# The last steps of a graph layer on one core: stores of the output without an order, and the work behind the last gather in another order

## The chip, the cores and the metric

The kernel runs on one core of a Trainium2 chip. The core has a matrix engine (TensorE, in the profile PE, with PEld for the loads of its stationary operand), a vector engine (VectorE, DVE), a scalar engine (ScalarE, ACT), GpSimd (POOL) and a sync engine (SyncE, SP), each with an instruction stream of its own; 16 DMA engines move data between the chip's DRAM and its SBUF. PE writes into PSUM, eight banks of 2 KB per partition, from which DVE and ACT read. The metric is the device time of one execution in microseconds (us); less is better. The time before the change is the median of three runs.

## What is computed

A graph attention layer over N = 12500 nodes of 256 features (HID) in 8 heads of D = 32, and E = 200000 edges sorted by their target `dst`. `src` gives the edge's other end.

```python
h = relu(layernorm(x))                                  # over the 256 features
q, k, v = h @ Wq + bq, h @ Wk + bk, h @ Wv + bv         # per node, 8 heads of 32
logits = einsum('ehd,ehd->eh', q[dst], k[src]) / sqrt(32)
expv = exp(logits - segment_max(logits, dst)[dst])
attn = expv / segment_sum(expv, dst)[dst]
agg = segment_sum(attn[:, :, None] * v[src], dst)
y = h + gelu(agg.reshape(N, 256) + h @ Wskip + bskip)
out = x + layernorm(y) * gamma + beta
```

## The kernel before

**Stages.** `project` computes h, k and v for all nodes and writes them to tables in DRAM (`h_tab`, `kv_tab`); beside it `make_plan` prepares the edges. Then `walk_streams` walks the edges, and this is nearly all of the time. The list of edges is cut into S = 8 streams of 25000, and 66 steps (NST) each take 383 edges of every stream, in K = 3 tiles of 128 edges. The last step, 65, has two tiles. An edge's row of `kv_tab` is gathered by an indirect DMA on POOL (`gather_row`, L1041), 128 rows at a time, eight for a tile; the tile lies in a buffer named `kv`, of which there are six.

**A step** c, for its tiles j:

- `spread` (L1092, PE) spreads the queries of the step's window of nodes over the edges; `times` (L1102, DVE) multiplies by k, in two halves; `total` (L1109, DVE) sums to logits.
- `turn` (L1125, PE) turns the logits of tile j into the bank `ps_x`, the one bank for the logits and the weights of all steps; `maxima` (L1137 to L1140 on DVE, then the exponential, L1141, on ACT) finds the maximum of each node and takes the exponential; `turn_back` (L1147, PE) turns the weights back into the same bank.
- `weights` (L1155, L1157, ACT) copies weights into the buffers `vw`, of which there are three; `weigh` (L1164, DVE) multiplies v by the weights into `vw`; for tile 0 there is L1169 besides.
- `hot_n` (L1082, ACT, behind a product on PE) makes `to_n`, which says which edge belongs to which node. There is one buffer for it.
- `add_up(c, i)` (L1183, PE) sums the weighted rows by node, in three groups i of streams: group 0 has the four streams with a narrow window (32 nodes), groups 1 and 2 two wide ones (64) each. ACT copies the sums to SBUF (L1193, one copy for a group) and hands each stream's open node on to the next step, one copy for a stream (L1199: four, two and two). SP stores the sums to `table` (L1203): four, two and two stores.

The stages of two steps are interleaved by hand: while step c is weighed and added up, the logits of step c + 1 are made.

**Finished nodes** are taken in pairs of blocks of 128 nodes (`Pair`), a pair in about four of five steps from step 10 on; pair 45 is the one that is started in step 64. A pair goes through `fetch` (SP: sums from `table`, x, and h), `turn` (h transposed on PE, L825, and copied by ACT to `hT`, L828), `skip` (h @ Wskip, on PE: bias L838 and eight products L842), `divisors` and `divide` (DVE, L817 to L831), `add` (PE adds the quotient to the skip product, L847), `gelu` (ACT, L851), `stats` (DVE, L854 to L860), `root` (ACT, L864), `factors` (DVE), `normal` (ACT, L874), `shifted` (PE, x + beta, L881 and L884), `scale` (DVE, L888 and L890: the result) and two `store` (SP, L895). ACT needs the table of Gelu, of Sqrt or of Exp for three of these functions; `table_of` (L963) calls for one ahead of its use with a one-element dummy.

**The last four pairs**, 46 to 49, can only be summed when the last step is done. They are of the class `Last`: x and h are fetched early (`fetch_rows`, L918 and L919), into two `kv` buffers that no gather needs any more, two pairs in each; the sums come behind the last store to `table` (`find_sums` reads the places, `fetch_sums`, L926, loads). Their skip products lie in the four banks `ps_qe`, which are those of `spread`. Two further pairs are behind a branch that isn't taken with these inputs.

**What sets the order.** Buffers, semaphores and waits are placed by a framework, from the tiles that each instruction reads and writes. It serializes writes into one DRAM tensor whose place is known only at run time, as the stores to `out` are; `table` has a place per stream. The order of the instructions on PE, DVE, ACT and SP is that of the program's text: `keep` ties each instruction to the one before it on its engine.

Behind the loop, in step 65, the text before does in this order: `hot_n`, `maxima`, pair 45's quotient, `turn_back`, `weights`, `weigh` of tile 0, pair 45 up to gelu, the first last pair's `turn`, `add_up` of tile 0, `weigh` of tile 1, `add_up` of tile 1, `skip` of the first last pair, the fetch of the sums, the rest of pair 45, `turn` and `skip` of the other three, the stores of the two pairs in flight, then the last four pairs from `divisors` on, stage by stage.

## Time and profile before

| what | value |
|---|---|
| time, median of 3 runs | 2327.23 us (2321.52 to 2327.32) |
| the profiled execution's own time | 2328.28 us |
| its span, first to last instruction | 2326.5 us |
| DVE busy | 1922.8 us, 83% |
| PE busy | 1816.3 us, 78% |
| POOL busy | 1561.7 us, 67% |
| ACT busy | 1066.4 us, 46% |
| DMA engines, mean rate over the span | 257 GB/s |
| mean granted clock of PE | 0.889 |
| last gather issued (POOL) | at 2241.76 us |

The span is cut by the loop: up to about 2242 us the gathers run, and from there to the end, 84 us, is the stage that the change is about. Rows of the instructions in order of time begin with the start in us from the span's start and the duration in us; then engine, line, operation, what is written and read, shape and count. In brackets stands how long the engine was idle before it and what ended that. A row with a count covers several instructions in a row, from the first's start. Rows by source line give minimum, median and maximum duration in ns, and the first and last start.

### The profile page before, as it was taken

To read this page: it belongs to the slowest core of one execution; us is meant where nothing else is said; L and a number is where in the kernel's file an instruction comes from. 1 tells how busy PE (TensorE), PEld (TensorE's weight loads), DVE (VectorE), ACT (ScalarE), POOL (GpSimd) and SP (SyncE) were. 2 spreads that over 40 slices of the span, in tenths; PEclk is the share of its full clock that TensorE was granted. 3 is DMA by queue.
4 is the path that set the end of the run, shared out by engine and by line. 5 is a ranking of instruction groups with operands and counts; after the bars stand their busy time and mean duration, and the time that the engine had idled before them with its cause. 6 is when DMAs were issued, how large, how long until landed. Compare 5 with 4: busy or idle time off the path is not lost.

```text
span 2326.5 us, 36089 instructions
## 1 busy us (share of the span) xinstructions
PE 1816.3 (78%) x10196; PEld 1070.9 (46%) x10196; DVE 1922.8 (83%) x2205; ACT 1066.4 (46%) x2517; POOL 1561.7 (67%) x1648
## 2 busy tenths in 40 slices
PE   7899666677788788788788788788787888788775
PEld 3444334444445454445454444455454545445443
DVE  8889477777888888888899888888898888799874
ACT  3432223333355455455455455455454555455453
POOL 2220677777777777777777777777777777777740
PEclk9999778888798899898899899898899899899887
DMA  7866788888889899898988888998998898898871
GB/s 285 290 243 222 238 235 244 243 244 243 260 267 277 258 275 276 263 274 266 274 272 271 264 267 264 270 274 261 275 277 265 266 274 264 263 276 267 265 214 54
DMA packets 275990, 597.92 MB, mean 257 GB/s; under 512 B 52295, under 2 KB 166164, under 8 KB 273600
## 3 DMA queue, kind: packets, MB, share of 16 engines
q0 software_dynamic: 128768, 423.23, 60.7%
q1 hardware_dynamic: 146482, 171.81, 22.7%
q8 instruction: 84, 1.38, 0.2%
q14 instruction: 126, 1.03, 0.1%
q10 hardware_dynamic: 530, 0.47, 0.1%
HBM read 512.83 MB, written 82.47 MB: 256 GB/s over the span
## 4 chain that ended last, share of the span: by engine, by line
PE 35%; DMA 23%; DVE 17%; ACT 12%; issue 7%; POOL 5%; SPq 1%; DVEq 0%; ACTq 0%; POOLq 0%
DMA kv<-kv_tab,idx 21%; DVE vw L1164 7%; PE ps_qe L1092 6%; PE ps_kv L250 5%; PE ps_a L1183 5%; PE ps_hot L1183 4%; PE ps_hot L1021 4%; DVE L L1109 4%; PE ps_a L842 4%; DVE kv L1102 4%; POOL kv L1041 3%; ACT kv L1199 3%; ACT to_n L1082 3%; PE ps_a L847 1%; ACT sums_w L1193 1%
## 5 line engine op out<-in xcount | busy, mean ns | idle before, releaser
L1041 POOL DMA_INDIRECT kv<-kv_tab,idx x1528 | 1471.5, 963 | 465.5 <-issue 220.3
L1102 DVE TENSOR_TENSOR kv<-ps_qe,kv 128x1024 f32<-128x1024 f32 x394 | 471.5, 1220 | 270.4 <-DMA kv<-kv_tab,idx 167.4
L1092 PE MATMUL ps_qe<-qw,to_e 64*128 64x256 f32 x3152 | 454.1, 420 | 108.3 <-DVE kv L1102 78.9
L1164 DVE TENSOR_TENSOR vw<-ps_x,kv 128x2048 f32<-128x2048 f32 x197 | 449.5, 2282 | 28.8 <-ACT vw L1157 28.1
L1109 DVE TENSOR_REDUCE L<-kv 128x64 f32<-128x2048 f32 x197 | 450.0, 2284 | 5.2
L1092 PEld LDWEIGHTS ps_qe<-qw,to_e 64*128 64x128 f32 x3152 | 328.6, 203 | 246.8 <-issue 150.1
L1024 ACT COPY qw<-ps_hot 128x256 f32<-128x256 f32 (+1 forms) x132 | 63.3, 479 | 429.7 <-PE ps_hot L1021 429.7
L1183 PE MATMUL ps_a<-vw,to_n 128*32 128x264 f32 (+1 forms) x2344 | 245.4, 441 | 11.2 <-ACT kv L1199 10.8
L1007 ACT COPY hwT<-ps_hot 128x256 f32<-128x256 f32 (+1 forms) x132 | 63.5, 481 | 343.9 <-PE ps_hot L1003 343.7
L1021 PE MATMUL ps_hot<-w_q,hwT 128*128 128x256 f32 x792 | 212.1, 405 | 1.0 <-ACT hwT L1007 0.8
L250 PE MATMUL ps_kv<-w_kv,hT 128*128 128x512 f32 x392 | 185.1, 615 | 22.9 <-ACT hT L143 22.0
L1021 PEld LDWEIGHTS ps_hot<-w_q,hwT 128*128 128x128 f32 x792 | 143.3, 194 | 82.2 <-issue 57.2
L1125 PE MATMUL ps_x<-ident,L 128*64 128x128 f32 x197 | 60.5, 307 | 151.4 <-DVE vw L1164 135.7
L963 ACT ACT_TABLE_LOAD x138 | 177.1, 1283 | 2.5
L1183 PE MATMUL ps_hot<-vw,to_n 128*64 128x264 f32 x808 | 155.2, 540 | 1.8 <-DVE o L890 1.8
L1183 PEld LDWEIGHTS ps_a<-vw,to_n 128*32 128x32 f32 (+1 forms) x2344 | 101.9, 130 | 98.1 <-issue 28.7
L1199 ACT COPY kv<-ps_a 1x264 f32<-1x264 f32 x388 | 143.2, 369 | 6.4
L1070 ACT ACTIVATE to_e<-ps_hot,ones 128x384 f32<-128x384 f32 x264 | 142.2, 582 | 6.2 <-DMA wide<-gvu_d 6.1
L1193 ACT COPY sums_w<-ps_a 128x264 f32<-128x264 f32 x130 | 49.3, 379 | 180.7 <-PE ps_a L1183 177.7
L842 PE MATMUL ps_a<-w_s,hT 128*128 128x256 f32 x368 | 120.4, 484 | 14.8 <-ACT hT L828 13.7
L250 PEld LDWEIGHTS ps_kv<-w_kv,hT 128*128 128x128 f32 x392 | 71.7, 193 | 105.5 <-issue 70.6
L1067 PE MATMUL ps_hot<-et,near 48*128 48x384 bf16 x264 | 86.5, 328 | 41.3 <-ACT qw L1024 26.6
(282 smaller groups left out, 2103.5 us busy)
## 6 DMA issues: line engine op xcount, KB each, us to landing
kv<-kv_tab,idx POOLq DMA_INDIRECT x1576
kv_tab<-kvo SPq DMA_DIRECT2D x14, 1536.0 KB
hw<-h_tab SPq DMA_DIRECT2D x264, 64.0 KB
table<-sums_w SPq DMA_DIRECT2D x264, 61.9 KB
pen<-pen_tab SPq DMA_DIRECT2D x66, 192.5 KB
sums<-table SPq DMA_DIRECT2D x92, 132.0 KB
x_f<-in_x_dram SPq DMA_DIRECT2D x92, 128.0 KB
h<-h_tab SPq DMA_DIRECT2D x92, 128.0 KB
```

The costliest lines, as they stand in the source:

```text
L250: ins = nc.tensor.matmul(ps_kv, hT[:, c, :], w_kv[:, c, :], start=c == 0, stop=c == KC - 1)
L842: self.keep(nc.tensor.matmul(self.ps[:, b, :], self.hT[:, b, c, :], w_s[:, c, :], start=False, stop=False, skip_group_check=True))
L963: keep(nc.scalar.activation(dummy[:, 1:2], dummy[:, 0:1], function))
L1021: keep(nc.tensor.matmul(ps[:, b, :], g["hwT"][:, b, k, :], w_q[:, k, :], start=False, stop=k == KC - 1, skip_group_check=True))
L1041: ins = nc.gpsimd.indirect_dma_start(out=t[:, s, :], out_offset=None, in_=kv_tab[:, :], in_offset=bass.IndirectOffsetOnAxis(ap=idx[:, s, j ...
L1070: keep(nc.scalar.activation(step[c]["to_e"][:, i, :], ps[:, :CH], AF.Relu, scale=-1.0, bias=ones))
L1092: keep(nc.tensor.matmul(ps[:, b, a, :], g["to_e"][r, 2 * half + a, j * P:(j + 1) * P], g["qw"][r, (half + a) * half, :], start=True, stop= ...
L1102: keep(nc.vector.tensor_tensor(k, g["qe", half].rearrange("p b a d -> p a b d"), k, op=OP.mult))
L1109: keep(nc.vector.tensor_reduce(g["L"][:, j, :].rearrange("p (s h) -> p s h", s=S), g["kv"][j][:, :, :HID].rearrange("p s (h d) -> p s h d" ...
L1164: keep(nc.vector.tensor_tensor(t[:, :, HEADS:].rearrange("p s (h d) -> p s h d", h=HEADS), wj[:, :, :, None].to_broadcast([P, S, HEADS, D] ...
L1183: keep(nc.tensor.matmul(ps[at:at + w, :], g["to_n"][:, j, i * P + at:i * P + at + w], g["vw"][j][:, s, :], start=j == 0, stop=j == tiles_o ...
L1199: keep(nc.scalar.copy(step[c + 1]["kv"][0][0:1, s, HID - HEADS:], ps[at:at + 1, :]))
```

## The change

Three things are changed, all in `walk_streams`.

1. The stores to `out` are declared free of dependencies on one another (two blocks of nodes can overlap, and a node's row is the same in both). This holds for all pairs.
2. In step 64 the rows of the first two last pairs are fetched earlier in SP's order, ahead of the turn of step 64's last logits; their `turn` and `skip` stand ahead of the weighing of step 64's tile 1 and of the turn of step 65's tile 1.
3. What stands behind the loop is put into another order. Step 64 breaks off after the weighing of its last tile. Then come the Exp table, `add_up(64, 0)`, `maxima(65)`, `add_up(64, 1)`, `turn_back(65)`, `add_up(64, 2)`, `hot_n(65)`; tile 1 is weighed before `weights`, then pair 45 up to the quotient, then tile 0. Each group is added up for both tiles at once. Pair 44 (`older`) and pair 45 (`pair`) go through `stats` to `scale` together, so that one Sqrt table serves both; the third last pair's `turn` and `skip` stand between `root` and `factors`, the fourth's behind the next Gelu table. `products` allocates the `vw` buffers apart from `weights`.

No arithmetic is added or removed; behind the start of step 64 there is one load of a table less on ACT (a Sqrt).

```diff
         def store(self, b):
...
-            self.keep(nc.sync.dma_start(out[ds(self.nodes[b], P), :], self.y[:, b, :]))
+            ins = self.keep(nc.sync.dma_start(out[ds(self.nodes[b], P), :], self.y[:, b, :]))
+            tc.declare_no_dep(ins.ins, group="stores", reason="a node's row is the same in every block")
+            tc.add_to_no_dep_group("stores", ins.ins)
...
+        def products(c):
+            step[c]["vw"] = [work.tile([P, S, SUMS], F32, name="vw", bufs=K) for _ in range(K)]
...
             if c:
                 weigh(c - 1, K - 1)
                 gather_next(c - 1, K - 1)
+            if c == NST - 2:
+                for i in range(2):
+                    last(i)
             if c + 2 < NST:
                 turn_windows(c + 2, 0)
             turn(c, K - 1)
...
             if c == NST - 2:
-                for i in range(4):
+                for i in range(2, 4):
                     last(i)
...
             total(c + 1, 1)
+            if c == NST - 2:
+                for p in lasts[:2]:
+                    p.turn()
+                    p.skip()
             weigh(c, 1)
             gather_next(c, 1)
             turn(c + 1, 1)
...
             if c == NST - 2:
                 weigh(c, K - 1)
-                add_up(c, 0, range(K - 1, K))
-                add_up(c, 1)
-                if pair_next:
-                    pair_next.turn()
-                    pair_next.skip()
+                older, pair, before = pair, pair_next, None
+                break
             if pair:
                 table_of(AF.Sqrt)
                 pair.stats()
                 pair.root()
                 table_of(AF.Exp)
-            if c == NST - 2:
-                add_up(c, 2)
...
         c = NST - 1
+        n = tiles_of(c)
+        table_of(AF.Exp)
...
+        add_up(c - 1, 0, range(K - 1, K))
+        maxima(c)
+        add_up(c - 1, 1)
+        turn_back(c)
+        add_up(c - 1, 2)
+        for j in range(n):
             hot_n(c, j)
+        products(c)
+        for j in range(1, n):
+            weigh(c, j)
+        weights(c)
         if pair:
+            pair.turn()
+            pair.skip()
             pair.divisors()
             pair.divide()
         weigh(c, 0)
+        table_of(AF.Gelu)
         if pair:
             pair.add()
             pair.gelu()
+        if older:
+            older.stats()
         for p in lasts:
             p.find_sums()
         for i in range(3):
+            add_up(c, i, range(n))
         for p in lasts:
             p.fetch_sums()
         if pair:
             pair.stats()
+        table_of(AF.Sqrt)
+        for p in (older, pair):
+            if p:
+                p.root()
+        for p in lasts[2:3]:
             p.turn()
             p.skip()
+        for p in (older, pair):
+            if p:
+                p.factors()
+                p.normal()
+        for p in (older, pair):
+            if p:
+                p.shifted()
+        table_of(AF.Gelu)
+        for p in lasts[3:]:
+            p.turn()
+            p.skip()
+        for p in (older, pair):
             if p:
+                p.scale()
                 p.store(0)
                 p.store(1)
```

More of the change, by code (lines that the diff above doesn't have):

```diff
@@ L1149, in turn_back @@
             turns(latest[PE])
+        def products(c):
+            step[c]["vw"] = [work.tile([P, S, SUMS], F32, name="vw", bufs=K) for _ in range(K)]
         def weights(c):
             g = step[c]
-            g["vw"] = [work.tile([P, S, SUMS], F32, name="vw", bufs=K) for _ in range(K)]
+            if "vw" not in g:
+                products(c)
             keep(nc.scalar.copy(wden[c % 2][0:1], g["kv"][0][0:1, :, HID - HEADS:HID]))
@@ L1374, in walk_streams @@
         c = NST - 1
-        for j in range(tiles_of(c)):
-            if tiles_of(c) == K and j < 2:
-                times(c, K - 1, j)
-            hot_n(c, j)
-            if tiles_of(c) == K and j == 1:
-                total(c, K - 1)
-        if tiles_of(c) == K:
-            turn(c, K - 1)
-        maxima(c)
+        n = tiles_of(c)
+        table_of(AF.Exp)
+        if n == K:
+            for half in range(2):
+                times(c, K - 1, half)
+            total(c, K - 1)
+            turn(c, K - 1)
+        add_up(c - 1, 0, range(K - 1, K))
[4 more added lines that the diff above has]
+        for j in range(n):
+            hot_n(c, j)
+        products(c)
+        for j in range(1, n):
+            weigh(c, j)
+        weights(c)
         if pair:
-            table_of(AF.Gelu)
+            pair.turn()
+            pair.skip()
             pair.divisors()
             pair.divide()
-        if before:
-            before.factors()
-        turn_back(c)
-        weights(c)
         weigh(c, 0)
+        table_of(AF.Gelu)
         if pair:
@@ L1395, in walk_streams @@
             pair.gelu()
-        if before:
-            before.normal()
-            before.shifted()
-        for p in lasts[:1]:
-            p.turn()
-        for j in range(1, tiles_of(c) - 1):
-            weigh(c, j)
-        for i in range(3):
-            add_up(c, i, range(tiles_of(c) - 1))
-        weigh(c, tiles_of(c) - 1)
+        if older:
+            older.stats()
         for p in lasts:
@@ L1408, in walk_streams @@
         for i in range(3):
-            add_up(c, i, range(tiles_of(c) - 1, tiles_of(c)))
-        for p in lasts[:1]:
-            p.skip()
-        if before:
-            before.scale()
+            add_up(c, i, range(n))
         for p in lasts:
@@ L1417, in walk_streams @@
             pair.stats()
-            pair.root()
-            pair.factors()
-            pair.normal()
-            pair.shifted()
-            pair.scale()
-            table_of(AF.Gelu)
-        for p in lasts[1:]:
+        table_of(AF.Sqrt)
[3 more added lines that the diff above has]
+        for p in lasts[2:3]:
             p.turn()
             p.skip()
-        for p in (before, pair):
+        for p in (older, pair):
             if p:
+                p.factors()
[10 more added lines that the diff above has]
+                p.scale()
                 p.store(0)
```

## The prediction

> **What bounds the kernel now.** First the head of the page, and the busy time by stretches of the last stage.
>
> ```profile
> span 2326.5 us, 36089 instructions
> ...
> 2310.00:2327.00 17.00, 0.00 (x0) 0.00 (x0) 0.00 (x0) 0.00 (x0) 0.00 (x0) 0.50 0.14 43
> ```
>
> The profiled run took 2328.28 us: its span and 1.78 us around it, 1.05 us over the median of the runs (2327.23). In the last 17 us no engine computes. So I read there the instructions in order of time (of SP too), the rows of the output's stores by tile, SP's waits, and the rows of the program's last line.
>
> ```profile
> 2309.29 0.69 DVE L890 TENSOR_TENSOR kv<-kv,ps_hot 128x512 f32<-128x512 f32 x1 [0.41 <-PE ps_hot L884]
> ...
> 2303.40 17.13 SPq L895 DMA_DIRECT2D out_dram<-kv  x8
> ...
> L895 SPq DMA_DIRECT2D out_dram<-kv x8: 332/332/333, 2303.4 to 2320.2; - x8
> ...
> SPq L895 <- DMA out_dram<-kv: 13.1, 7, 3.0
> ...
> L1800 SPq EVENT_SEMAPHORE  x14: 17/28/28, 2324.9 to 2326.4; - x14
> ```
>
> The last result is ready at 2309.29 + 0.69 = 2309.98. The eight stores of the last four pairs run from 2303.4 to 2320.2, 2.4 us apart, and seven of them waited 13.1 us in all for the store before. From the last issue to the end are 2326.5 - 2320.2 = 6.3 us: the landing, the branch, and from 2324.9 the meeting of the engines. These 6.3 us stay.
>
> Next the instructions from the turned logits of step 65 (tile 1) to the first quotient that is added.
>
> ```profile
> 2252.89 0.42 PE L1125 MATMUL ps_x<-ident,L 128*64 128x128 f32 x1 [4.97 <-DVE vw L1164]
> ...
> 2253.35 2.29 DVE L1164 TENSOR_TENSOR vw<-ps_x,kv 128x2048 f32<-128x2048 f32 x1 [0.51 <-PE ps_x L1125]
> ...
> 2255.70 1.11 PE L1183 MATMUL ps_a<-vw,to_n 128*32 128x264 f32 x8 [0.47 <-DVE vw L1164]
> ...
> 2256.90 0.38 ACT L1193 COPY sums_w<-ps_a 128x264 f32<-128x264 f32 x1 [8.40 <-PE ps_a L1183]
> ...
> 2257.17 1.55 ACT L1199 COPY kv<-ps_a 1x264 f32<-1x264 f32 x4
> ...
> 2258.58 0.42 DVE L1140 TENSOR_TENSOR W<-ps_x,M 64x256 f32<-64x256 f32 x1
> ...
> 2262.58 1.56 PE L1183 MATMUL ps_hot<-vw,to_n 128*64 128x264 f32 x12
> ...
> 2266.19 0.41 ACT L1141 ACTIVATE W<-W 64x256 f32<-64x256 f32 x1
> ...
> 2268.38 2.29 DVE L1164 TENSOR_TENSOR vw<-ps_x,kv 128x2048 f32<-128x2048 f32 x1 [5.68 <-ACT vw L1157]
> ...
> 2276.07 2.03 PE L1183 MATMUL ps_hot<-vw,to_n 128*64 128x264 f32 x8
> ...
> 2276.26 0.38 ACT L1193 COPY sums_w<-ps_a 128x264 f32<-128x264 f32 x1 [4.40 <-PE ps_a L1183]
> ...
> 2278.18 0.38 ACT L1193 COPY sums_w<-ps_hot 128x264 f32<-128x264 f32 x1 [0.50 <-PE ps_hot L1183]
> ...
> 2282.29 5.61 SPq L926 DMA_DIRECT2D kv<-table  x8
> ...
> 2285.03 0.17 DVE L817 TENSOR_SCALAR den<-kv 128x16 f32<-128x16 f32 x1 [1.82 <-DMA kv<-table]
> ...
> 2289.64 0.18 DVE L817 TENSOR_SCALAR den<-kv 128x16 f32<-128x16 f32 x1 [0.24 <-DMA kv<-table]
> ...
> 2291.87 1.03 PE L847 MATMUL ps_qe<-kv,ident 128*128 128x256 f32 x4
> ```
>
> DVE has nothing for 5.68 us before 2268.38: step 65 is weighed late, because its exponential ran at 2266.19 although its argument was there at 2258.58 + 0.42 = 2259.00. On ACT it stood behind all copies of step 64's sums, a turned h and two table loads. Step 65's sums are complete on PE at 2278.10 and copied at 2278.56, the table is read back from 2282.29, and the first quotient is added on PE at 2291.87, though its sums were there at 2285.03: PE was still at skip products of later pairs.
>
> **The change part by part.** Prices, from the instructions in order of time:
>
> ```profile
> 2204.92 4.57 SPq L1203 DMA_DIRECT2D table<-sums_w  x8
> ...
> 2247.65 0.27 PE L1125 MATMUL ps_x<-ident,L 128*64 128x128 f32 x1
> ...
> 2248.11 0.33 SPq L812 DMA_DIRECT2D h<-h_tab  x1
> ...
> 2258.82 0.66 PE L825 MATMUL ps_hot<-ident,h 128*128 128x128 f32 x4
> ...
> 2259.57 0.69 DVE L831 TENSOR_TENSOR o<-sums,den 128x512 f32<-128x512 f32 x1 [0.21 <-DVE den L819]
> ...
> 2260.02 0.59 ACT L828 COPY hT<-ps_hot 128x512 f32<-128x512 f32 x1
> 2260.62 1.28 ACT L963 ACT_TABLE_LOAD   x1
> ...
> 2265.25 1.05 ACT L1082 ACTIVATE to_n<-ps_hot,ones 128x384 f32<-128x384 f32 x2
> ...
> 2268.25 0.58 ACT L851 ACTIVATE sums<-ps_a 128x512 f32<-128x512 f32 x1
> ...
> 2280.60 1.09 ACT L874 ACTIVATE sums<-sums,nm,rstd 128x256 f32<-128x256 f32 x2 [0.43 <-DVE nm L869]
> 2280.78 1.13 PE L884 MATMUL ps_hot<-x_f,ident 128*128 128x256 f32 x4
> ...
> 2283.72 1.99 PE L842 MATMUL ps_qe<-w_s,hT 128*128 128x256 f32 x8 [1.05 <-ACT hT L828]
> ```
>
> *Two skip products ahead of the turned logits.* PE is free from 2247.65 + 0.27 = 2247.92 to 2252.89. A pair costs there 0.66 (transposes), 0.59 (copy on ACT, which is free), 1.99 (eight products) and some 0.05 between: 3.3 us; two end at 2254.5. The turned logits end at 2254.8 instead of 2253.31, and step 64's third weighing, which waited 0.51 for them before too, runs from 2254.85 to 2257.15 instead of 2255.64: 1.5 us lost on the path. In return two skip products leave the row in front of 2291.87.
>
> Those logits lie in other columns than the weights that DVE reads, and yet PE waited 4.97 us at 2252.89 for a weighing, and DVE for PE behind it. The Trainium skill, PSUM — Partial Sum Buffer, section PSUM bank collisions raise a hardware error, says that accesses of two engines are to be kept apart by bank, not by address. By this rule, with which the trace agrees, the 1.5 us are lost; by address the weighing could start at 2252.9, and the sum would be some 1.3 us better.
>
> *Exponential ahead of copies.* Step 64's first group of sums is complete 1.11 us after 2257.15 (PE's last eight products, as at 2255.70), at 2258.3; its copies (1.9 us, 2256.90 to 2257.17 + 1.55) stay in front: 2260.2. DVE's scans are done at 2259.0 as before, so the exponential ends at 2260.6 instead of 2266.60. The Sqrt table and root no longer stand before it, and the Exp table (1.28 and the dummy) is loaded while ACT is empty, about 2253. Then on PE the turned weights (0.35) and the third group of sums, 1.56, to 2262.5. That frees the buffer into which tile 1 is weighed: 2262.5 to 2264.8. ACT meanwhile: copies of two groups to 2263.6, to_n 1.05 to 2264.65, the copy of weights behind the weighing to 2265.1. Pair 45: hT to 2265.7, skip 1.99 to 2267.75, add 1.13 (four products against ident, as the shifted x) to 2268.9, gelu 0.58 to 2269.5; its Gelu table fits beside the skip. DVE has divisors and quotient (1.3) to 2266.1 and tile 0 to 2268.6, under PE's 2269.5, which must leave the bank first.
>
> *Sums in one go.* 32 products: 16 narrow ones and 16 wide ones. Wide ones at 1.56 / 12 are 2.1 us, at the rate of 2276.07 (eight in 2.03) 4.1; the narrow ones half of that. PE has little idle time there, so I take the first, 3.1 us: 2272.6, against 2278.10; the other would be 3 us worse. Gain by here 5.5 us. Its first copy ends at 2271.0; eight table stores and the fetch start 5.65 later, as before (2276.26 + 0.38 to 2282.29): 2276.7. Sums of the first pair arrive at 2279.4, of the last at 2284.0 (2.74 and 7.35 later, as 2285.03 and 2289.64).
>
> *The rest.* ACT: last copy 2273.0, Sqrt table and dummy 1.5, two roots, hT of the third pair: 2275.6. PE: its skip to 2277.7, two shifted x (1.45 each with the bias) to 2280.6, transposes of the fourth pair, hT on ACT (four normals, twice 1.09, and the Gelu table are done at 2279.3), skip: 2283.9. DVE scales pairs 44 and 45 by 2281.3 and has the first quotient at 2282.6, under PE's 2283.9. So the first add starts at 2283.9 instead of 2291.87: 8.0 us less, 2.5 more than by the sums. What follows to the last result, 2309.98 - 2291.87 = 18.1 us, is unchanged: 2302.0.
>
> *Stores in any order.* The last two go out at 2302.0 and 2302.6 (0.6 us each, as eight table stores in 4.57), not at 2320.2: 17.6 less, of which 9.6 would come with the old order of work (2309.98 and one 0.6 for 2320.2). The end: 2302.6 + 6.3 = 2308.9. In the loop such waits are next to nothing (the last row of the next fence), and nothing is taken for them.
>
> *Eight loads moved ahead.* SP takes them once the weighing in front frees their buffer, for 4.6 us. Behind them on SP stand one store, eight table stores and the six loads of pair 45, which went out till 2248.4 and now till some 2253; landing 2.7 us later they are 8 us ahead of that pair's transposes (2264). Taken at nothing; the engines that they share are in a rival below.
>
> Sum: +1.5 - 7.0 (sums), - 2.5 (skip products), - 9.6 (stores) = **-17.6 us**. 2328.28 - 17.6 = 2310.7; from the median 2309.6. Forecast **2310.0**.
>
> **The rivals.**
>
> ```profile
> 2211.63 3.78 PE L842 MATMUL ps_a<-w_s,hT 128*128 128x256 f32 x8
> ...
> 2248.35 2.29 DVE L1109 TENSOR_REDUCE L<-kv 128x64 f32<-128x2048 f32 x1
> ...
> 2236.00:2240.00 4.00, 3.77 (x27) 2.04 (x24) 3.90 (x6) 3.05 (x10) 3.09 (x4) 0.81 0.83 255
> ...
> L895 SPq DMA_DIRECT2D out_dram<-o x92: 333/361/399, 652.1 to 2294.6; - x92
> ...
> SPq L895 <- DMA out_dram<-o: 7.7, 5, 3.1
> ```
>
> *A: something holds up the turned logits.* At 2211.63 eight skip products took 3.78 instead of 1.99. Two pairs at that rate end 4.3 us later (1.8 each, and slower transposes), and all behind with them: -13.3, **2314**. For it: PE pauses for each copy of hT. Against it: it is otherwise busy from 2244 on. The other way are the last gathers. Between 2236 and 2240 the DMA engines are busy to 0.83 with 255 GB/s, so at most some 307 GB/s; eight loads of 128 KB are 1.05 MB, 3.4 us. If all of it delays the last gather, the reduction at 2248.35 and the weighing behind (2.3 us each) end at 2256.3, 1.8 us after the skip products: **2312**. The Trainium skill, DMA: Bandwidth & Descriptors, section Issuing engines are not separate DMA queues, says that DMAs of all issuers run on the same 16 engines and interleave; by it the delay is somewhere from nothing to those 3.4 us.
>
> *B: the order of the stores stays* (another dependency, or a limit of stores in flight). The first result is then there at 2303.4 - 8.0 = 2295.4, the eight stores take 16.8 us to 2312.2, the end is 2318.5 and the time **2319.3**. Against it: eight table stores went out in 4.57 us.
>
> *C: slower.* SP waits no more for a loop's store, so that wait could fall on DVE's product that writes o again (L831), in each of 46 pairs (92 stores). To end over 0.3% slower it must eat the 17.6 and 7 us more, 0.53 us a pair: **2334** and more. It decides where a store lands later than o is reused, two pairs on. 92 stores from 652.1 to 2294.6 are a pair every 36.5 us, and SP's five waits were 3.1 us at most, so I see no such store.
>
> **How the numbers follow.** A measurement of this kernel can tell some 0.3%, 7 us, from no change: under 2320.2 is faster. As summed, 2306 to 2312: 0.60. A by either way, 2312 to 2316: 0.19. B, 2317 to 2323: 0.10. C: 0.03. Quicker than summed (the buffer free before the third group's end, full clock in every group), 2301 to 2306: 0.08. The low end, 2304.0, is the sum without the 1.5 us and with 4 us of such gains; the high end, 2318.0, takes in all of A, its two ways together and the slow products of step 65 (3 us) in part. Left out are C, most of B and part of the quickest. Half of B lies under the bound: faster is 0.92 by these cases, 0.90 with a little for a mishap not seen; same 0.06, slower 0.04.
>
> **What would show it.** SP has no store that waits for a store, and the last one leaves within 1 us of the last result. The turned logits of step 65, tile 1, end near 2254.8, behind PE's skip products and not behind DVE. The exponential runs near 2260, behind five copies; tile 1 is weighed before tile 0 and after step 64's third group of sums; the fetch starts near 2276.7, the first add at 2284. The forecast is wrong if the last stores stand 2 us apart, if the granted clock falls under 0.7 between 2248 and 2256, if products of step 65, tile 1, wait for a gather, or if pairs of the loop wait at L831.

## The result and the profile after

| | before | after |
|---|---|---|
| time, median | 2326.07 us (2321.52 to 2327.32, 6 runs) | 2308.2 us (2305.89 to 2314.78, 6 runs) |
| after / before | | 0.9933, 95% interval 0.9916 to 0.9949 |
| profiled execution, its span | 2328.28, 2326.5 us | 2307.75, 2306.0 us |

By the ratio the time is 15.6 us (11.9 to 19.5) less; the medians are 17.9 us apart. The first fence has the head of the page and the instructions in order of time, after the change, from the products of step 65, tile 1, to the last result. The lines are those of the kernel after: the logits are turned in L1127, weighed in L1171, summed in L1190.

```profile
span 2306.0 us, 36086 instructions
...
2238.80 3.78 PE L842 MATMUL ps_a<-w_s,hT 128*128 128x256 f32 x8
...
2244.66 2.36 DVE L1104 TENSOR_TENSOR kv<-ps_qe,kv 128x1024 f32<-128x1024 f32 x2 [2.55 <-PE ps_qe L1094]
...
2251.07 1.99 PE L842 MATMUL ps_qe<-w_s,hT 128*128 128x256 f32 x8 [0.41 <-ACT hT L828]
...
2252.90 0.27 PE L1127 MATMUL ps_x<-ident,L 128*64 128x128 f32 x1
...
2253.21 2.29 DVE L1171 TENSOR_TENSOR vw<-ps_x,kv 128x2048 f32<-128x2048 f32 x1 [1.68 <-PE ps_x L1127]
...
2258.07 0.41 ACT L1143 ACTIVATE W<-W 64x256 f32<-64x256 f32 x1
...
2258.79 1.56 PE L1190 MATMUL ps_hot<-vw,to_n 128*64 128x264 f32 x12
...
2259.51 2.29 DVE L1171 TENSOR_TENSOR vw<-ps_x,kv 128x2048 f32<-128x2048 f32 x1 [2.10 <-PE ps_hot L1190]
...
2266.99 1.10 PE L1190 MATMUL ps_a<-vw,to_n 128*32 128x264 f32 x16 [0.69 <-ACT sums L851]
...
2268.02 2.00 PE L1190 MATMUL ps_hot<-vw,to_n 128*64 128x264 f32 x16
...
2270.07 0.38 ACT L1200 COPY sums_w<-ps_hot 128x264 f32<-128x264 f32 x1 [0.51 <-PE ps_hot L1190]
...
2274.23 5.62 SPq L928 DMA_DIRECT2D kv<-table  x8
...
2280.55 1.03 PE L847 MATMUL ps_qe<-kv,ident 128*128 128x256 f32 x4
...
2288.44 0.17 DVE L868 RECIPROCAL rstd_l<-rstd_l 128x2 f32<-128x2 f32 x1 [2.41 <-ACT rstd_l L864]
...
2297.97 0.69 DVE L890 TENSOR_TENSOR kv<-kv,ps_hot 128x512 f32<-128x512 f32 x1 [0.41 <-PE ps_hot L884]
```

In order: PE finishes the second skip product and at once turns the logits, for which DVE has waited 1.68 us. Tile 1 of step 65 is weighed at 2259.51, 6.30 us behind step 64's last weighing (15.03 before, 2268.38 - 2253.35), and DVE waits there for PE's sums, which free the buffer, no longer for ACT's exponential. The sums themselves wait 0.69 us for pair 45's gelu on ACT, which must leave their bank first. They are copied by 2270.45, the first quotient is added at 2280.55, the last result is there at 2298.66.

Now the rows of the last stores (by tile, of the kernel after) and those of two lines, the branch and the program's end.

```profile
2292.07 9.41 SPq L895 DMA_DIRECT2D out_dram<-kv  x8
...
L895 SPq DMA_DIRECT2D out_dram<-kv x8: 332/332/850, 2292.1 to 2301.1; - x8
...
L1464 SPq EVENT_SEMAPHORE  x9: 17/17/17, 2298.6 to 2300.3; - x9
...
L1464 SPq COMPARE_BRANCH  x1: 58/58/58, 2298.4 to 2298.4; - x1
...
L1814 SPq EVENT_SEMAPHORE  x14: 17/28/28, 2304.3 to 2305.9; - x14
```

No store waits for a store any more. But the last one stands 2.5 us behind the last result, and in front of it SP is in the line of the branch over the two further pairs, from 2298.4 to 2300.3. In the text this branch comes behind all stores.

**Where the time went.** Whole spans say little here. Call T the start of the products of step 65, tile 1 (2244.66 above). Six of the traces below have the same program up to there (after, e0_again, c0_control, e3_branch_last, e9_tail, e10_tail_branch), and T lies anywhere from 2240.22 to 2250.89 in them. From T on the kernel repeats to within a few tenths, but for groups of PE's products that fall into a half clock. So every run is compared from T. All numbers are differences of rows like those above: from T to the last weighing of step 64 (X), from X to the end of the last copy of sums (C), to the first addition (A), to the last result (R), and to the end of the span.

| run | T to X | X to C | C to A | A to R | R to end | sum |
|---|---|---|---|---|---|---|
| before | 7.39 | 25.21 | 13.31 | 18.11 | 16.52 | 80.54 |
| after | 8.55 | 17.24 | 10.10 | 18.11 | 7.34 | 61.34 |
| e0_again (as after) | 8.55 | 17.93 | 10.10 | 18.10 | 7.23 | 61.91 |
| c0_control (as after) | 8.59 | 17.23 | 10.10 | 18.11 | 7.21 | 61.24 |
| e1_stores | 7.38 | 25.21 | 13.31 | 18.11 | 7.24 | 71.25 |
| e2_order | 8.37 | 17.26 | 11.74 | 18.10 | 16.57 | 72.04 |
| e3_branch_last | 8.41 | 17.26 | 10.10 | 18.10 | 8.25 | 62.12 |
| e11_half_again | 8.40 | 18.92 | 10.09 | 18.11 | 7.16 | 62.68 |
| e9_tail | 8.40 | 18.93 | 10.10 | 17.49 | 6.86 | 61.78 |
| e10_tail_branch | 8.81 | 17.25 | 11.74 | 17.45 | 5.33 | 60.58 |
| e4_skips_back | 7.39 | 17.88 | 16.41 | 18.12 | 10.26 | 70.06 |
| e6_exp_behind | 8.40 | 19.58 | 10.09 | 18.11 | 7.22 | 63.40 |
| e7_half_loads | 8.40 | 18.92 | 11.76 | 18.11 | 7.60 | 64.79 |
| e8_branch_early | 8.41 | 18.93 | 11.69 | 18.65 | 5.98 | 63.66 |

Before to after: +1.16 - 7.97 - 3.21 + 0 - 9.18 = -19.20 us. Where X to C is some 18.9 (19.58 in e6_exp_behind), and where C to A is some 11.7, one pair's skip products in that stretch took 3.0 to 3.7 us instead of 1.99, and in some traces the products behind them took longer too; it costs 1.65 us. No edit causes it: e9_tail and e10_tail_branch have the same program up to A, and one has the slow products ahead of C, the other behind. In e0_again twelve sums took 2.91 instead of 1.56, and in e4_skips_back 2.64, for 0.6 to 0.7 us.

The times say somewhat less than these 19.2 us: 15.6 (11.9 to 19.5) here, 18.1 and 17.7 in the two repeats below. The start T doesn't settle the rest: it lies at 2245.96 before and at 2246.85 in e1_stores, and at 2246.7 in the mean of the six.

The last four runs of the table were made on a chip whose granted clock was lower (0.82 by mean, against 0.89 to 0.90); their times, 2755 to 2765 us, are compared only with the kernel before on that chip, 2779 us. The stretches above agree all the same.

### The profile page after: what moved, and what is told of

It is laid out like the page before. It is cut to its first block, busy times and chain, and to the rows that moved or that the text cites. A ratio compares the mean times of both kernels' runs of the same rounds, so it can differ in the third digit from the quotient of the medians.

```text
span 2306.0 us, 36086 instructions
## 1 busy us (share of the span) xinstructions
PE 1807.7 (78%) x10196; PEld 1067.8 (46%) x10196; DVE 1922.0 (83%) x2205; ACT 1065.2 (46%) x2516; POOL 1559.1 (68%) x1648
## 4 chain that ended last, share of the span: by engine, by line
PE 33%; DMA 27%; DVE 15%; ACT 12%; issue 7%; POOL 5%; SPq 0%; DVEq 0%; POOLq 0%; ACTq 0%
DMA kv<-kv_tab,idx 23%; DVE vw L1171 6%; PE ps_qe L1094 6%; PE ps_a L1190 5%; PE ps_kv L250 5%; PE ps_hot L1190 5%; DVE L L1111 4%; PE ps_hot L1023 4%; PE ps_a L842 4%; DVE kv L1104 3%; ACT kv L1206 3%; POOL kv L1043 3%; ACT to_n L1084 3%; DMA e_tab<-row 2%; ACT sums_w L1200 1%
## 5 line engine op out<-in xcount | busy, mean ns | idle before, releaser
L1171 DVE TENSOR_TENSOR vw<-ps_x,kv 128x2048 f32<-128x2048 f32 x197 | 449.5, 2282 | 24.1 <-ACT vw L1164 20.0
L1111 DVE TENSOR_REDUCE L<-kv 128x64 f32<-128x2048 f32 x197 | 450.0, 2284 | 5.2
L1190 PE MATMUL ps_a<-vw,to_n 128*32 128x264 f32 (+1 forms) x2344 | 243.0, 437 | 12.9 <-ACT kv L1206 10.9
L1127 PE MATMUL ps_x<-ident,L 128*64 128x128 f32 x197 | 60.4, 307 | 147.7 <-DVE vw L1171 132.1
L1190 PE MATMUL ps_hot<-vw,to_n 128*64 128x264 f32 x808 | 151.0, 528 | 0.0
L1190 PEld LDWEIGHTS ps_a<-vw,to_n 128*32 128x32 f32 (+1 forms) x2344 | 100.9, 129 | 98.2 <-issue 26.3
L1206 ACT COPY kv<-ps_a 1x264 f32<-1x264 f32 x388 | 143.2, 369 | 6.3
L1200 ACT COPY sums_w<-ps_a 128x264 f32<-128x264 f32 x130 | 49.3, 379 | 174.1 <-PE ps_a L1190 171.3
```

Of the source, the lines that this page charges most:

```text
L1111: keep(nc.vector.tensor_reduce(g["L"][:, j, :].rearrange("p (s h) -> p s h", s=S), g["kv"][j][:, :, :HID].rearrange("p s (h d) -> p s h d" ...
L1171: keep(nc.vector.tensor_tensor(t[:, :, HEADS:].rearrange("p s (h d) -> p s h d", h=HEADS), wj[:, :, :, None].to_broadcast([P, S, HEADS, D] ...
L1190: keep(nc.tensor.matmul(ps[at:at + w, :], g["to_n"][:, j, i * P + at:i * P + at + w], g["vw"][j][:, s, :], start=j == 0, stop=j == tiles_o ...
L1206: keep(nc.scalar.copy(step[c + 1]["kv"][0][0:1, s, HID - HEADS:], ps[at:at + 1, :]))
```

## The experiments

The theories are told with each run. Where a run tests a part of the forecast, theory 1 is that this part (the stores' order, the exponential's place, the skip products) brings or costs what was reckoned; the others are its rivals. Runs made together are compared with the same executions of the kernel before.

**The change once more**, twice, without an edit, as the measure for the others.

> The changed kernel once more. In its first profile the products of step 65, tile 1, start 17.2 us after the third weighing of step 63 starts, against 14.5 before the change; the skip product of pair 44 took 3.78 us there instead of 1.99. Theory 1 (chance: the phase in which PE's clock is lowered): the distance is 14.5 to 15 again in this run if that skip product runs at full clock. Theory 2 (the eight loads moved ahead delay gathers and with them PE): 17 us again. The tail from the first quotient added to the last result is 18.1 us, and the last store goes out 2.4 us behind the last result, in both.

> The changed kernel once more, as the control of the three runs beside it. Both theories expect 0.992 to 0.995 of the kernel before; from the first addition to the last result 18.1 us, from there to the end 7.3.

Measured: 2310.84 us, ratio 0.9922 (0.9902 to 0.9942), and 2312.8 us, ratio 0.9924 (0.991 to 0.9938). With the first comparison, three measurements lie between 0.9922 and 0.9933. The distance in question was 13.9 us in e0_again, where pair 44's skip products took 1.99 us, and 17.1 in c0_control, where they took 3.78 again, with the same program: theory 1 holds. The last store goes out 2.5 and 2.3 us behind the last result.

**The stores alone**: the kernel before, with the declaration.

```diff
-            self.keep(nc.sync.dma_start(out[ds(self.nodes[b], P), :], self.y[:, b, :]))
+            ins = self.keep(nc.sync.dma_start(out[ds(self.nodes[b], P), :], self.y[:, b, :]))
+            tc.declare_no_dep(ins.ins, group="stores", reason="a node's row is the same in every block")
+            tc.add_to_no_dep_group("stores", ins.ins)
```

> The kernel before with the stores' declaration alone. Theory 1 (the order of the stores cost only the tail): the result is ready as before, some 57 us after the third weighing of step 64 starts; the last store goes out some 2 to 2.5 us behind the last result, because SP's branch is put ahead of the last two stores and waits there for all landings; the end follows 4.9 us later. Gain 7.7 + 1.4 = some 9 us, ratio 0.996. Theory 2 (the loop loses or wins by it too): the start of step 64's third weighing moves by more than the 4 us by which runs of one kernel differ, and the ratio is under 0.994 or over 0.999.

**The order alone**: the kernel after, with the old line in place of those three.

> The changed kernel without the stores' declaration: the new order of work alone. Theory 1: the first quotient is added some 25 us after the third weighing of step 64 ends, as in the changed kernel (36 before), then 18.1 us to the last result, and the eight stores stand 2.4 us apart again: last store 10 us behind the last result, end 6.3 us later. Gain 8 to 11 us, ratio 0.996. Theory 2 (the order of the stores held up more than the tail): gain under 5 us.

Measured: the stores alone 2318.4 us, 0.9955 (0.9938 to 0.9972); the order alone 2315.19 us, 0.9955 (0.9939 to 0.9972). SP's waits, first of the order alone, then (the stores' rows by tile) of the stores alone:

```profile
SPq L895 <- DVE o L890: 358.7, 43, 14.3
SPq L895 <- DMA out_dram<-kv: 13.1, 7, 3.0
```

```profile
L895 SPq DMA_DIRECT2D out_dram<-kv x8: 332/332/844, 2304.3 to 2313.3; - x8
```

With the dependency seven stores wait 13.1 us, the same as before the change, and R to the end is 16.57 us; without it 7.24, in the old order of work as in the new. In the table each run has the stretches of the part that it holds, and the others of the kernel before: the parts are independent, and 80.54 - 71.25 = 9.29 and 80.54 - 72.04 = 8.50 (10.15 without its one slow skip product) are together 17.8 (19.4 without it), against the change's 19.2. The times agree within their noise: twice 0.0045 is 0.009, and e0_again, measured beside them, has 0.0078 (0.0058 to 0.0098); the first comparison's 0.0067 (0.0051 to 0.0084) lies a little lower. The rival that the stores keep some order falls.

**The branch behind the stores**: the stores of the two pairs behind the branch stay outside the group, so that they, and the branch, must stay behind the others.

```diff
             ins = self.keep(nc.sync.dma_start(out[ds(self.nodes[b], P), :], self.y[:, b, :]))
+            if not self.free:
+                return
             tc.declare_no_dep(ins.ins, group="stores", reason="a node's row is the same in every block")
```

> The changed kernel, but the stores of the two pairs behind the branch stay ordered, so that the branch stays behind all stores. Theory 1 (the 2.4 us between the last result and the last store are SP's branch, which waits for landings): the last store goes out 0.6 us behind the last result, and from there to the end are 6.3 us again instead of 4.9; the sum is 0.4 us better or equal. Theory 2 (SP waits for a free place for a DMA): the last store is still 2 us or more behind the last result.

Measured: 2311.85 us, 0.9932 (0.9916 to 0.9949). The stores' rows by tile, and the branch's by line:

```profile
L895 SPq DMA_DIRECT2D out_dram<-kv x8: 332/333/846, 2291.3 to 2298.4; - x8
```

```profile
L1466 SPq EVENT_SEMAPHORE  x9: 17/17/17, 2299.0 to 2301.8; - x9
```

The last store goes out 0.55 us behind the last result (2297.85), as predicted for the change, and the branch's nine semaphore instructions come behind it, up to 2301.8. So it is the branch that held the last two stores, and the declaration that let it pass them. But from there to the end are 7.7 us, not the 6.3 expected, and R to the end is 8.25, 0.9 more than after: the branch's 2 to 3 us, first spent beside the last product, now follow the last store. The expected gain of the earlier store is not there; why the 7.7 us are more than before the change is open.

**The branch ahead of the last statistics.** Here the block `if extra:` stands in front of the last `table_of(AF.Sqrt)`.

> The changed kernel with the branch over the two further pairs put ahead of the last four pairs' statistics, where SP has nothing to do. Theory 1 (the branch is on SP's way to the end): the last store goes out 0.6 us behind the last result and the end follows 4.8 us later, 5.4 us in all instead of 7.3; from the first quotient to the last result it is still 18.1 us. Theory 2 (each engine has to run empty at the branch): these 18.1 us grow by 2 us or more, and nothing is won.

Measured: 2761.76 us against 2779.46, 0.9937 (0.9909 to 0.9966). R to the end is 5.98 us (5.4 were expected), 1.2 to 1.4 less than after and its repeats; A to R is 18.65, 0.5 more, since PE and ACT cross the branch between the additions and gelus. Together 24.63 us against 25.32 to 25.45: 0.7 to 0.8 us, too little for a time to show.

**The two skip products back at the third's place**, as before the change.

```diff
-            if c == NST - 2:
-                for p in lasts[:2]:
-                    p.turn()
-                    p.skip()
...
-        for p in lasts[2:3]:
+        for p in lasts[:3]:
```

> The changed kernel with the skip products of the first two last pairs taken from in front of the turned logits to where the third's stand. Theory 1 (they cost about 1 us there and save two skip products later): step 64's third weighing starts 7.4 us after the products of step 65, tile 1 (8.4 to 8.6 in the changed kernel), and the first quotient is added some 16.5 us after the last copy of sums ends instead of 10.1, two pairs of 3.2 us: 5 us worse in all. Theory 2 (the last gather, late by the loads moved ahead, holds up the logits anyway): the third weighing still starts 8.4 us after, and the kernel is 6 us worse. Theory 3 (the skip products find idle PE time in the tail): under 2 us worse.

Measured: 2764.81 us, 0.9955 (0.9937 to 0.9972). The instructions in order of time, from the last weighing of step 64 on:

```profile
2710.73 2.29 DVE L1171 TENSOR_TENSOR vw<-ps_x,kv 128x2048 f32<-128x2048 f32 x1 [0.52 <-PE ps_x L1127]
...
2731.01 1.99 PE L842 MATMUL ps_qe<-w_s,hT 128*128 128x256 f32 x8 [1.93 <-ACT hT L828]
...
2734.11 1.99 PE L842 MATMUL ps_qe<-w_s,hT 128*128 128x256 f32 x8 [0.36 <-ACT hT L828]
...
2737.28 1.99 PE L842 MATMUL ps_qe<-w_s,hT 128*128 128x256 f32 x8 [0.41 <-ACT hT L828]
...
2743.19 1.99 PE L842 MATMUL ps_qe<-w_s,hT 128*128 128x256 f32 x8 [0.41 <-ACT hT L828]
...
2745.02 1.03 PE L847 MATMUL ps_qe<-kv,ident 128*128 128x256 f32 x4
```

T to X is 7.39 again and DVE's wait for the turned logits 0.52, as before: the +1.16 is the skip products. All four pairs' now stand between the last copy of sums and the first addition: C to A is 16.41, 6.3 more. So their early place costs 1.0 to 1.2 and saves 6.3 in the new order of work, as theory 1 has it. The old order lost only 3.2 there, since the first of the four stood ahead of the fetch of the sums. R to the end is 10.26 in this run; the row of SP's waits at the branch has 3.4 us in one piece, and why is open.

**Half of the early loads**: of the first two late pairs only h is loaded early, x behind the loads of the others.

```diff
         def fetch_rows(self):
             for b, node in enumerate(self.nodes):
-                self.keep(nc.sync.dma_start(self.x[:, b, :], x[ds(node, P), :]))
                 self.keep(nc.sync.dma_start(self.h[:, b, :], h_tab[ds(node, P), :]))
+        def fetch_x(self):
+            for b, node in enumerate(self.nodes):
+                self.keep(nc.sync.dma_start(self.x[:, b, :], x[ds(node, P), :]))
```

> The changed kernel with only the four loads of h moved ahead, the four of x behind those of the other two pairs. Theory 1 (the loads moved ahead take DMA time from the last gather): the second half of the products of step 65, tile 1, waits under 0.5 us (1.2 in the second run of the changed kernel, 1.0 with the order alone, 0 in the kernel before), and step 64's third weighing starts 8.0 us after the first half, set by PE's skip products, instead of 8.4 to 8.6. Theory 2 (the wait is not from the loads): it is still 1 us. In the whole time neither can be seen.

> The changed kernel, with only the four loads of h of the first two late pairs moved ahead, their x loaded behind (as e7_half_loads). Theory 1 (the turned logits wait for PE's skip products, the early loads cost nothing on the path): within 0.1% of the control, the second half of the products of step 65, tile 1, waits for no gather in either. Theory 2 (the early loads share the DMA engines with the last gather): the control shows a wait for the gather of 1.0 to 1.2 us, as e0_again and e2_order did, this run shows half of it or none, and the turned logits come up to 0.5 us earlier.

Measured: 2761.33 us, 0.9951 (0.9935 to 0.9967), and 2311.26 us, 0.9925 (0.991 to 0.9939), the latter beside the control's 2312.8. T to X is 8.40 in both, not the 8.0 that theory 1 of the first expected. Neither shows a wait for the gather, but the control and the other runs of the slower chip don't either, so the waits alone don't tell. They come where pair 44's skip products took 1.99 us and PE was early: then the second half of the products waited 1.0 to 1.5 us for the gather (e0_again, e2_order, e10_tail_branch), with the eight loads in front. (In e2_order the view puts this wait down to PE's bias product L838, which writes another buffer; the gather's last report is at 2243.02, the products start at 2243.10.) The rows of e0_again, in order of time:

```profile
2238.94 0.95 POOL L1043 DMA_INDIRECT kv<-kv_tab,idx  x1 [0.30 <-DMA kv<-kv_tab,idx]
2239.36 0.34 SPq L920 DMA_DIRECT2D kv<-in_x_dram  x1
...
2247.76 0.96 POOL L1043 DMA_INDIRECT kv<-kv_tab,idx  x1 [0.31 <-issue]
2250.89 1.22 DVE L1104 TENSOR_TENSOR kv<-ps_qe,kv 128x1024 f32<-128x1024 f32 x1
2253.31 1.22 DVE L1104 TENSOR_TENSOR kv<-ps_qe,kv 128x1024 f32<-128x1024 f32 x1 [1.21 <-DMA kv<-kv_tab,idx]
```

And the same of the stores alone, where those loads come late:

```profile
2233.71 0.95 POOL L1043 DMA_INDIRECT kv<-kv_tab,idx  x1 [0.30 <-issue]
...
2242.53 0.96 POOL L1043 DMA_INDIRECT kv<-kv_tab,idx  x1 [0.30 <-PE ps_hot L825]
...
2246.85 2.35 DVE L1104 TENSOR_TENSOR kv<-ps_qe,kv 128x1024 f32<-128x1024 f32 x2
```

The first and last of the gather's eight parts are 8.8 us apart in both, so POOL is not slowed by the loads (the first of which goes out behind the first part). In e0_again the second half begins 4.59 us behind the end of POOL's last part; in the other it did not wait, so its 4.54 (half of 2.35 behind 2246.85) is only a bound. But the trace also keeps the time at which the DMA engines report a part as moved. By the last report of each part (the rows here don't have it), the gather's last part landed 4.51 us behind POOL in e0_again and 3.65 in the stores alone; the mean of all eight parts is:

| run | loads in front of the last gather | landing, mean of eight parts |
|---|---|---|
| before, e1_stores | none | 3.23, 3.42 us |
| e11_half_again | four | 3.96 |
| the seven with all eight, on the faster chip | eight | 4.23 to 5.26 |

Of the loop's last hundred gathers, those with complete reports (68 to 84 in a run) have 3.4 to 3.6 in the median, and a fifth to three tenths of them 4.2 or more. So a single trace tells nothing, but all seven lie there. The loads do stretch the landing, by 0.8 to 2 us, as theory 2 of e11_half_again has it. Little of it reaches the path: in e0_again 1.2 us of the wait come from POOL's first part, which starts 1.98 us behind the start of step 63's last weighing (2236.96) against 0.79 (2232.92), before a load was issued; and the turned logits wait for the skip products anyway. By these alone (the end of the second and 0.15 us, as in after) X could have come 0.4 to 0.65 us earlier in the three traces; this is an estimate, not a run. T to X is 8.37 to 8.81 in all eleven traces with the early skip products, whichever of the two waits ends last.

**The exponential behind the copies**: all three groups of step 64 are added up and copied first.

```diff
         add_up(c - 1, 0, range(K - 1, K))
-        maxima(c)
         add_up(c - 1, 1)
-        turn_back(c)
         add_up(c - 1, 2)
+        maxima(c)
+        turn_back(c)
```

> The changed kernel with all copies of step 64's sums ahead of the exponential. Theory 1 (the exponential's place in front of four copies is worth what stands in front of it, less what runs beside it): the weighing of step 65, tile 1, starts 8.2 us after the third weighing of step 64 starts instead of 6.3, and the first quotient is added 1.6 to 2 us later. Theory 2 (the way over the copies, to_n and pair 45's transposes is as long, so that the place is worth nothing): under 0.5 us at the first quotient.

Measured: 2755.15 us, 0.993 (0.991 to 0.995).

```profile
2697.00 2.29 DVE L1171 TENSOR_TENSOR vw<-ps_x,kv 128x2048 f32<-128x2048 f32 x1 [1.53 <-PE ps_x L1127]
...
2703.97 0.41 ACT L1143 ACTIVATE W<-W 64x256 f32<-64x256 f32 x1
...
2704.81 2.29 DVE L1171 TENSOR_TENSOR vw<-ps_x,kv 128x2048 f32<-128x2048 f32 x1 [3.61 <-PE ps_x L1149]
...
2707.89 3.68 PE L842 MATMUL ps_a<-w_s,hT 128*128 128x256 f32 x8 [1.30 <-ACT hT L828]
```

The exponential starts 4.7 us behind the end of step 64's last weighing (2699.29), against 2.6 after and 10.5 before. Tile 1 is weighed 1.5 us later than after (7.81 behind X against 6.30), but X to C is 19.58, and 1.7 of that is the skip product of 3.68: some 17.9, 0.65 more than after, between the two theories. The place ahead of these copies (six of them: two of L1200, four of L1206) is worth that little, presumably since copies that are done early are not in the way of pair 45's turned h later. Of the 8.0 us by which the exponential moved up, 2.1 are this place; the other 5.9 go with what no longer stands in front of it on ACT (by the rows of before: the Sqrt table and root, a turned h, `to_n`, and the Exp table, which is now loaded earlier, while ACT is idle). No run takes these away one by one.

**The tail behind the first addition.** It did not change: 18.1 us in every run so far but e8_branch_early. Two orders in it looked to matter: the first two of the last pairs share a bank, so that PE's second addition waits for the first gelu, and DVE is idle for 2.41 us in front of the first reciprocal (L868, 2288.44 above) though statistics are still to be made.

```diff
-                if i % 2 == 0:
-                    banks[i // 2] = qe_ps.tile([P, 2, 2, HID], F32, name="ps_qe")
-                return banks[i // 2][:, i % 2]
+                if i < 2:
+                    banks[i] = qe_ps.tile([P, 2, 2, HID], F32, name="ps_qe")
+                return banks[i % 2][:, i // 2]
...
             p.gelu()
+        for p in lasts:
+            p.stats()
         table_of(AF.Sqrt)
         for i in range(len(lasts) + 2):
             if i < len(lasts):
-                lasts[i].stats()
                 lasts[i].root()
```

> The changed kernel with two edits behind the first addition, where the change altered nothing: the first and second of the late pairs get PSUM buffers of their own (PE's second addition then doesn't wait for the first gelu), and the statistics of all four pairs stand ahead of the Sqrt table (DVE was idle for 2.41 us in front of L868 there). Theory 1 (those 18.1 us are set by these two orders): 15.0 to 16.5 us from the first addition to the last result, 2 to 3 us less time than the control. Theory 2 (they are set by ACT's gelus, table and roots, or by PE's shifted x, which waits 3.27 us for a result's buffer): 17 to 18.1 us, within 1 us of the control.

And the same with the branch in the place of e8_branch_early:

> As e9_tail, and the branch over the two further pairs stands ahead of the last statistics, as in e8_branch_early. Theory 1 (without the order of the stores the branch is what holds the last two stores and the end): from the last result to the end 6.0 us instead of 7.3, of which some 0.5 is given back at the first result; 0.5 to 1.3 us less than e9_tail. Theory 2 (the branch costs the same wherever it stands): the same as e9_tail within 0.3 us from the first addition to the end.

Measured: 2308.21 us, 0.9906 (0.9891 to 0.9921), and 2308.67 us, 0.9911 (0.9896 to 0.9926), beside the control's 0.9924 (0.991 to 0.9938). The tail with the first edits, in order of time:

```profile
2287.45 3.71 PE L847 MATMUL ps_qe<-kv,ident 128*128 128x256 f32 x16
...
2296.06 0.13 DVE L868 RECIPROCAL rstd_l<-rstd_l 128x2 f32<-128x2 f32 x1
...
2296.43 1.09 ACT L874 ACTIVATE kv<-kv,nm_l,rstd_l 128x256 f32<-128x256 f32 x2 [2.75 <-DVE nm_l L869]
...
2299.09 0.58 PE L881 MATMUL ps_hot<-b_o,one_row 3*128 3x512 bf16 x1 [5.18 <-DVE kv L890]
...
2304.25 0.69 DVE L890 TENSOR_TENSOR kv<-kv,ps_hot 128x512 f32<-128x512 f32 x1 [1.25 <-PE ps_hot L884]
```

The sixteen additions now run in 3.71 us without a pause, but A to R is 17.49, only 0.6 less. Two waits took the place of those removed: DVE makes all statistics before it turns to the first reciprocal, so ACT's first normal waits 2.75 us for it; and PE's third shifted x waits 5.18 us for a result to leave its buffer, and the last result then waits for PE. Of e9_tail's theories the second holds: 17.49 us lie in its 17 to 18.1. The branch's early place takes R to the end down to 5.33 us. From A to the end it is 24.35 and 22.78 us, against 25.32 of the control: 2.5 us less at best, 1.6 of them by the branch (0.5 to 1.3 were expected). That is what the traces show; the times of the three runs overlap, so no difference between the variants is measured.

## Why the prediction was right

The forecast was 2310.0 us; 2308.2 was measured. By its terms:

| step | predicted | measured | with |
|---|---|---|---|
| two skip products ahead of the turned logits | +1.5 | +1.16 | after; gone in e4_skips_back |
| sums of step 65 complete and copied earlier | -7.0 | -7.97 | after, e2_order |
| two skip products less ahead of the first addition | -2.5 | -3.21 | after, e3_branch_last |
| first addition to last result | 0 | 0.00 | all but the edited tails |
| stores in any order | -9.6 | -9.18 | after, e1_stores |
| sum | -17.6 | -19.20 | |

- **Turned logits**: DVE's weighing waited 1.68 us for logits that PE turns into other columns of its bank, and these for PE's skip products, as said (the Trainium skill, PSUM — Partial Sum Buffer, section PSUM bank collisions raise a hardware error, has accesses kept apart by bank; that the weighing may not start earlier agrees). Rival A's first way, a half clock in these products, did not come: both took 1.99 or 2.00 in every trace. A half clock (3.78 us) fell on pair 44's products just ahead (2238.80) and held up step 65's products themselves, 2.55 us. Pair 44's products took 3.1 to 3.8 us in five of the eight traces of the new order on the faster chip and 1.99 in both of the old; but 19 of the 46 such groups of the kernel before took over 2.5 us, so this is more likely the loop's chance than the change. Rival A's second way, the gathers, came in part: products of step 65, tile 1, waited 1.0 to 1.5 us for a gather in three later traces, which the prediction had named a sign of being wrong, and the loads do stretch that gather. But it was worth 0.4 to 0.65 us at X (the estimate above), not 1.8, since the skip products end at nearly the same time. The bound of 307 GB/s behind the 1.8 was too low: after moved 369 GB/s between 2236 and 2240.
- **Sums**: the buffer behind the third group of sums set tile 1's weighing, as forecast, though it came free 0.84 us ahead of that group's end (2260.35), and 16 wide products took 2.00 us, the faster of the two rates weighed (2.1). The sums then waited for pair 45's gelu, also as forecast, which ended 13.7 us behind X instead of 14.65 (2269.5 - 2254.85): this is nearly all of the 1.0 us by which the size was low. The reason was only partly right: the words "exponential ahead of copies" stand for little (0.65 us in e6_exp_behind). The exponential moved up by 8.0 us and the sums by as much. By the rows this is mostly what left ACT's queue in front of it (table loads, a root, a turned h, `to_n`), but how much of the gain each of these, and the adding up in one go, brings was not measured.
- **Stores**: the size was right by two errors. "The last two go out at 2302.0 and 2302.6" and "These 6.3 us stay" both failed: the last store stands 2.5 us behind the last result because the branch passed it on SP, and the end then follows its issue by 4.9 us, since the branch is already behind. The marker "the last one leaves within 1 us of the last result" was not met. Only e3_branch_last, with 0.55 and 7.7 us, has the order that was forecast.
- **Rivals B and C**: B fell with e1_stores. Of C there is no sign: DVE waited for nothing ahead of its 46 products that write `o` again (L831, by line, of after), and in e1_stores, the old order with free stores, T lay at 2246.85, within 0.9 us of before (T varies by 10 us, so this alone would prove little).

The Trainium skill, DMA: Bandwidth & Descriptors, section Anatomy of one DMA — SWDGE (gpsimd) path, gives a DMA issued by GpSimd a fixed cost of about 2.0 us, most of it the receipt of the write. Here, with stores issued by SP, a store that waits for another follows it by 2.4 us and one that doesn't by 0.5 to 0.6: the difference, 1.8 to 1.9, is near that.

The forecast of 2310.0 lies 1.8 us from the measured median, and this closeness is partly luck: by the marks the gain is 1.6 us more than the sum, by the ratio of the times 2.0 less.

## What to carry to other kernels

When a kernel ends in a chain of dependent stores, look whether the dependency is real: taking it away was worth as much as all of the reordering. Free instructions from an order, and other instructions may move too, a branch here; so look at what stands on the queue in front of the last one. And compare stretches between two marks of the trace, not spans, where a loop ahead of them varies by more than the edit.

## What was not expected of the hardware

The kernel before took 2779.46 us in one comparison, on one chip, and 2326 to 2329 in the three others. Rows of groups of instructions, by line and shape: skip products and the products by weights, after the change, then of e6_exp_behind on the slower chip.

```profile
L842 PE MATMUL ps_a<-w_s,hT 128*128 128x256 f32 x368 | 120.8, 485 | 14.3 <-ACT hT L828 13.0
...
L1171 DVE TENSOR_TENSOR vw<-ps_x,kv 128x2048 f32<-128x2048 f32 x197 | 449.5, 2282 | 24.1 <-ACT vw L1164 20.0 <-PE ps_hot L1190 2.1 <-PE ps_x L1127 1.7
```

```profile
L842 PE MATMUL ps_a<-w_s,hT 128*128 128x256 f32 x368 | 170.6, 643 | 9.1 <-ACT hT L828 3.5 <-issue 0.4
...
L1171 DVE TENSOR_TENSOR vw<-ps_x,kv 128x2048 f32<-128x2048 f32 x197 | 450.0, 2284 | 172.1 <-ACT vw L1164 140.5 <-PE ps_hot L1081 10.2 <-issue 7.7
```

DVE's product takes 2284 ns on the one and 2282 on the other, while one of PE's skip products takes 643 ns in the mean instead of 485, and DVE is idle 172.1 us in front of its weighings instead of 24.1. A group of eight takes 1.99 us or up to 3.78. Of the 46 such groups ahead of the last pairs, 45 or 46 took over 2.5 us in each trace of the slower chip, 16 to 26 in those of the other. The 3.78 us are those of pair 44 in the first fence of the result; busy times by stretches, after, with the granted clock as the last but two of the columns:

```profile
2240.00:2244.00 4.00, 4.00 (x15) 2.73 (x15) 2.11 (x3) 0.25 (x2) 0.73 (x1) 0.50 0.81 285
```

The granted clock is 0.50 there, and 1.00 between 2248 and 2256, where the groups took 1.99 us. The Trainium skill, TensorE: Matmul & The Clock Gate, section What's actually happening, has these two states, half and full rate, chosen by how busy the engine was in a short window; the two durations, 1.9 to 1, agree. Why one chip is in the lower state so much more often with the same program is open.
